# DMA transposes that read SBUF instead of a copy in DRAM, in a macaron block with an S4D layer

## The chip, the cores and the metric

The kernel runs on one core of a Trainium2 chip. The metric is the device time of one execution in microseconds (us). A core has a matrix engine (TensorE; PE in the profile, its weight loads PEld), a vector engine (VectorE, DVE), a scalar engine (ScalarE, ACT), GpSimd (POOL) and a sync engine (SP) that only issues transfers. Each has its own in-order queue of instructions; a DMA is issued from such a queue (SPq, ACTq, POOLq in the profile) and carried out by 16 DMA engines, which signal when the data has landed. SBUF is the on-chip memory of 128 partitions, PSUM holds what TensorE writes, and DRAM is off the chip's core.

## What is computed

The input `x` is 8 x 2048 x 256 in float32. Three sublayers follow each other, each added to its own input:

```python
x = x + 0.5 * ffn(layernorm(x))          # 256 -> 1024 (relu) -> 256
x = x + s4d(layernorm(x))                # below
x = x + 0.5 * ffn(layernorm(x))          # the same weights

# s4d, for each of the 256 channels h
K[h, l] = 2 * Re( sum_n Ct[h, n] * exp(dtA[h, n] * l) )       # 64 states, 2048 lags
y = causal convolution of the rows with K (the reference uses FFTs)
out = layernorm(x + y + x * D) * ln_w + ln_b
```

The kernel doesn't use FFTs. It cuts the 2048 positions into 16 chunks of 128 and computes the convolution by a table inside a chunk and by 64 complex states carried from chunk to chunk. For that it builds, for every pair of channels, tables of powers of exp(dtA) in two orientations: one is called P here, the other is P transposed.

## The kernel before, in words

**Sublayers.** The two feed-forward sublayers, `a` and `b`, run through the same function `sublayer`. A group `g` is 256 rows (two tiles of 128); there are 64 groups. A group takes 8 steps, one for each 128 of the 1024 hidden columns. In a step TensorE does six matmuls `up` (line 854: two halves of the depth times three products of high and low parts, by which float32 accuracy is reached), ACT makes the high part `hh` of the relu from PSUM (line 926), DVE the low part `hl` (line 116 is the helper that records it), and TensorE does the six matmuls `down` (line 864) of the step three steps earlier (`LAG = 3`). So ACT and DVE have about three steps to deliver a pair before TensorE stands still for it.

**Beside it**, generators advance by one `yield` in each step: `pre` prepares the rows of a later group (load, layer norm, transposition, split into `xh` and `xl`) and starts 18 (`a`) or 19 (`b`) steps before its group; `post` adds the result and, in sublayer `a`, normalizes the rows a second time into `u`, the input of the S4D layer. Most ACT and DVE instructions that are to keep their place in the queue are pinned behind what was traced before them (`keep_in_program_order`); the rest are ordered by the scheduler.

**Rows transposed in two ways.** Groups below `DMA_A = 44` in `a` and below `DMA_B = 2` in `b` are transposed on TensorE (line 794). The 20 groups of `a` from 44 on and the 62 groups of `b` from 2 on go through `turn_by_dma`: the float32 rows `xn` are split into two planes of 16-bit halves (`pl`, line 815, plane 0 on DVE, plane 1 on ACT), the planes are stored to DRAM (`xp`, line 819), three steps later a transposing DMA reads them back (`pt`, line 823), three steps after that DVE and ACT put the halves together again (`xf`, line 833, pinned), and `xh` and `xl` follow one and two steps later (lines 835 and 837). The tiles `pl`, `pt` and `xf` share one pair of buffers in rotation.

**The batches of P.** While sublayer `a` runs, a background generator (`matrices`) makes the tables. It is called at a pace in us: a cycle of its main loop is `PA = 9.1` of that pace in the first part and `PB_ = 10.3` in the second, cut into six sub-steps. There are 32 batches of 8 channels. In cycle `bt`, four generators advance together, each for its own batch:

- `make(bt)` computes P of the batch on POOL, six instructions, in place in a quarter of `u` that isn't filled yet (`room`).
- `spread(bt - 1)` waits two sub-steps (`DI`), copies the two 16-bit planes of P into `planes[:, bt % 2]` on ACT (line 620, pinned, one plane per sub-step, sub-steps 2 and 3), stores them to `pv_dram` (line 623, sub-step 4), and stores P itself to `o_dram` (line 625).
- `turn(bt - 2)` issues, at sub-step 2 of the next cycle, the transposing DMA from `pv_dram` back into the same half of `planes` (line 631, pinned on SP).
- `transpose(bt - 3)` puts the planes together again over P's own place (line 646: plane 0 on DVE, plane 1 on ACT, both pinned) at sub-step 0, and stores the result to `pt_dram` (line 650).

`planes` has two halves, taken in turn by the batches. The loop has 32 + `BACK` cycles with `BACK = 3`. A fourth generator, `lags`, runs along and makes the tables inside a chunk.

**After sublayer a** the states are computed from `pt_dram`, scanned over the chunks, and the outputs computed from `o_dram` (lines 1064 to 1178); then sublayer `b` follows.

Of the kernel before, what the change touches and what calls it, by code (L numbers as in the profile page):

```python
# [13 lines left out]
U16 = mybir.dt.uint16  # L14
# [5 lines left out]
P = 128  # L20
# [23 lines left out]
def macaron_s4d_kernel(  # L44
# [17 lines left out]
    nc = tc.nc  # L62
    V = nc.vector
    A_ = nc.scalar
# [3 lines left out]
    N = c_re.shape[1]  # L68
# [5 lines left out]
    NDC = H // P  # L74
    NFC = W // P
    NTB = 2
# [8 lines left out]
    PINT = 1  # L85
# [7 lines left out]
    BCH = 8  # L93
    NBT = H // BCH
# [6 lines left out]
    dram = ctx.enter_context(tc.tile_pool(name="dram", bufs=1, space=DRAM))  # L101
    ps = ctx.enter_context(tc.tile_pool(name="ps", bufs=2, space=PSUM))
    upool = ctx.enter_context(tc.tile_pool(name="upool", bufs=1))
    wpool = ctx.enter_context(tc.tile_pool(name="wpool", bufs=1))
# [4 lines left out]
    def bank(tag, name):  # L109
        return ps.tile([P, 512], F32, name=name, tag=tag, bufs=BANKS[tag])  # L110

    def slot(tag, shape, name, dtype=F32):
        return work.tile(shape, dtype, name=name, tag=tag, bufs=BUFS[tag])
# [99 lines left out]


    o_dram = [dram.tile([P, BCH * P], F32, name=f"o_{i}") for i in range(NBT)]
    pv_dram = [dram.tile([P, 2 * BCH * P], U16, name=f"pv_{i}") for i in range(2)]
    pt_dram = [dram.tile([P, BCH * P], F32, name=f"pt_{i}") for i in range(NBT)]
    kpad = dram.tile([H, KROW], F32, name="kpad")

# [38 lines left out]
    def matrices():  # L258
# [24 lines left out]
        for i, src in enumerate(raw + [dtx]):  # L283
            pt = bank("b", f"ptr{i}")
# [22 lines left out]
        r = zim  # L307
# [24 lines left out]
        f, a = r, z  # L332
# [133 lines left out]
        for i in range(H // P):  # L466
            nc.gpsimd.dma_start(
                out=kpad[i * P : (i + 1) * P, P + 1 :], in_=zeros[:, 0 : P - 1]
# [6 lines left out]
        with nc.allow_non_contiguous_dma(reason="256 numbers"):  # L475
            nc.gpsimd.dma_start(
                out=kpad.rearrange("(g c) k -> c g k", c=2)[:, :, P], in_=k0
# [100 lines left out]
        def p_of(bt):  # L578

            r, i = (room[2], 28 + bt % 4 * 8) if bt < first else (room[3], (16, 24, 48, 56)[bt % 4])  # L580
            return r[:, i * P : (i + 8) * P]
# [5 lines left out]
        def make(bt):  # L587

            E = G_
            pp = p_of(bt).rearrange("p (r g k) -> p r g k", r=2, g=PB)  # L590
            tm = tmp_of(bt)
            gs = slice(bt * PB, (bt + 1) * PB)
            br, bi = (
                pb[:, ri, gs, ::-1].unsqueeze(2).to_broadcast([P, PB, NA, NB]) for ri in range(2)
            )
            ar, ai = (
                pa[:, ri, gs, ::-1].unsqueeze(3).to_broadcast([P, PB, NA, NB]) for ri in range(2)
            )
            pr, pi = (pp[:, ri].rearrange("p g (a b) -> p g a b", b=NB) for ri in range(2))
            E.tensor_mul(pr, br, ar)  # L600
            yield
            E.tensor_mul(tm, bi, ai)
            yield
            E.tensor_sub(pr, pr, tm)
            yield
            E.tensor_mul(pi, br, ai)
            yield
            E.tensor_mul(tm, bi, ar)
            yield
            E.tensor_add(pi, pi, tm)  # L610
            yield

        def spread(bt):

            pl = planes[:, bt % 2]
            pu = p_of(bt).bitcast(U16).rearrange("p (m w) -> p w m", w=2)
            for _ in range(DI):
                yield
            for w in range(2):
                tc.keep_in_program_order(A_.copy(pl[:, w], pu[:, w]))  # L620
                yield
            via = pv_dram[bt % 2]
            nc.sync.dma_start(out=via, in_=pl.rearrange("p w m -> p (w m)"))
            yield
            nc.sync.dma_start(out=o_dram[bt], in_=p_of(bt))
            yield

        def turn(bt):
            for _ in range(PX):
                yield  # L630
            ins = nc.sync.dma_start(
                out=planes[:, bt % 2].rearrange("p w (k n) -> p (w k) n", n=P),
                in_=pv_dram[bt % 2], transpose=True,
            )
            if PINT:
                tc.keep_in_program_order(ins)
            yield

        def transpose(bt):
            pl, ptb = planes[:, bt % 2], p_of(bt)  # L640
            for _ in range(PY):
                yield
            pu = ptb.bitcast(U16).rearrange("p (c l r n w) -> p w r l c n", c=2, r=2, n=N, w=2)
            plv = pl.rearrange("p w (r l c n) -> p w r l c n", r=2, c=2, n=N)
            for w in range(2):
                ins = P_REINT[w](pu[:, w], plv[:, w])
                if PPIN:
                    tc.keep_in_program_order(ins)
            yield
            nc.sync.dma_start(out=pt_dram[bt], in_=ptb)  # L650
            yield

        planes = wpool.tile([P, 2, 2, BCH * P], U16, name="planes", tag="wE")
        P_REINT = (V.tensor_copy, A_.copy)
        PY = 0
        BACK = 3
        DI = 2
        PX = 2
        PA = 9.1
        PB_ = 10.3  # L660
        PPIN = 1

        beside = lags()
        for bt in range(NBT + BACK):
            parts = []
            if 0 <= bt - BACK < NBT:
                parts.append(transpose(bt - BACK))
            if 0 <= bt - 2 < NBT:
                parts.append(turn(bt - 2))
            if 0 <= bt - 1 < NBT:  # L670
                parts.append(spread(bt - 1))
            if bt < NBT:
                parts.append(make(bt))
            for n in range(6):
                for p in parts:
                    next(p, None)
                next(beside, None)
                yield (PA if bt < first + BACK else PB_) / 6
            if bt == first + BACK - 1:
                yield "half"  # L680
# [71 lines left out]
    def ffn_in(xt, name, on_act=NTB, by_dma=False, joint=None):  # L752
# [36 lines left out]
        if by_dma:  # L789
            return (yield from turn_by_dma(xn, name, Y2 - 1 if joint else Y2))  # L790
# [14 lines left out]
        V.tensor_sub(xl, ptv, xh.bitcast(F32))  # L805
        return xh, xl

    xp_dram = [dram.tile([P, 2 * NDC * NTB * P], U16, name=f"xp_{i}") for i in range(4)]

    def turn_by_dma(xn, name, y2):  # L810

        pl = slot("pl", [P, 2, NDC, NTB, P], f"pl_{name}", U16)
        xu = xn.bitcast(U16).rearrange("p i (d c w) -> p d i c w", d=NDC, w=2)
        for w, copy in DEINT:
            copy(pl[:, w], xu[:, :, :, :, w])  # L815
        yield
        via = xp_dram[turned_[0] % 4]
        turned_[0] += 1
        nc.sync.dma_start(out=via, in_=pl.rearrange("p w d i c -> p (w d i c)"))
        for _ in range(Y1):  # L820
            yield
        pt = slot("pl", [P, 2, NDC * NTB * P], f"pt_{name}", U16)
        nc.sync.dma_start(
            out=pt.rearrange("p w (k t) -> p (w k) t", t=P), in_=via, transpose=True
        )
        for _ in range(y2):
            yield
        xh = slot("xh", [P, NDC, TOK], f"xh_{name}", F32R)
        xl = slot("xl", [P, NDC, TOK], f"xl_{name}", F32R)
        xf = slot(XF, [P, NDC, TOK], f"xf_{name}")  # L830
        xv = xf.bitcast(U16).rearrange("p d (t w) -> p (d t) w", w=2)
        for w, copy in REINT:
            tc.keep_in_program_order(copy(xv[:, :, w], pt[:, w]))
        yield
        A_.copy(xh, xf)
        yield
        V.tensor_sub(xl, xf, xh.bitcast(F32))
        return xh, xl

    Y1, Y2 = 3, 3  # L840
    XF = "pl"
    DEINT = (0, V.tensor_copy), (1, A_.copy)
    REINT = (0, V.tensor_copy), (1, A_.copy)
    DMA_A = 44
    DMA_B = 2
    turned_ = [0]

    def up(wt, xT, ph, fc):
        xh, xl = xT
# [385 lines left out]
    def begin():  # L1235
        for _ in range(sizes[1] // PB):
            next(head)

    sublayer(
        w1t, w2t, pre_a, post_a, 18, "a", load_weights(), chain(matrices(), early()),  # L1240
        {"half": NG // 2, "tables": NG * 3 // 4},
        {NG * SLOTS - 6: lambda: next(head), NG * SLOTS - 1: begin},
# [127 lines left out]
```

## Time and profile before

| | |
|---|---|
| median of 3 runs | 1764.35 us (1762.26 to 1765.85) |
| the profiled execution's own time | 1761.45 us |
| its span, first to last instruction | 1759.6 us |
| TensorE busy | 1724.2 us, 98% |
| VectorE busy | 1373.7 us, 78% |
| ScalarE busy | 986.3 us, 56% |
| GpSimd busy | 588.7 us, 33% |
| moved by DMA | 242.68 MB; the SP queue's packets took 41.1% of 16 engines' span |
| transposing DMAs | 32 for P (`planes<-pv`), 20 and 62 for rows (`pt_a<-xp`, `pt_b<-xp`) |
| stores that feed them | 32 of 512 KB (`pv<-planes`), 82 of 256 KB (`xp<-pl`) |

Sublayer `a` lasts until about 806 us of the span, the S4D layer until about 1010, sublayer `b` to the end. The batches of P lie between 220 and 597 us.

In the rows of the profile, a name such as `planes<-pv` is output and input of a transfer, `L646` a line of the kernel, `x32` a count. In a table by windows each engine has its busy time and, in brackets, the number of its instructions in the stretch; PEclk is the TensorE clock that was granted, as a share of full speed, and the last two columns are the busy share of the DMA engines and what they moved in GB/s. In waits, the three numbers are us in total, times, and the longest. In the chain (the work that ended last, followed back from the end) the two numbers ahead are start and duration.

### The profile page before, as it was taken

What the parts mean: (1) busy time and instruction counts of PE and PEld (TensorE: products, weight loads), DVE (VectorE), ACT (ScalarE), POOL (GpSimd) and SP (SyncE); (2) the same over time, 40 slices, a digit from 0 to 9 for tenths busy, and PEclk for the clock granted to TensorE, in tenths of its full rate; (3) what the DMA queues carried; (4) which work ended last, traced back from release to release, by engine and by line L of the source; (5) the groups of instructions that cost most, each with busy time, mean ns of one, the idle gap of its engine ahead of it and who ended that gap; (6) DMA issues with size and microseconds to landing.
All of it is one profiled execution on the core that took longest, in us unless ns stands there. A gap on an engine that the chain in (4) does not pass through costs nothing.

```text
span 1759.6 us, 40994 instructions
## 1 busy us (share of the span) xinstructions
PE 1724.2 (98%) x15367; PEld 1697.3 (96%) x15367; DVE 1373.7 (78%) x4405; ACT 986.3 (56%) x2178; POOL 588.7 (33%) x550
## 2 busy tenths in 40 slices
PE   9999999989999999999999799999999999999998
PEld 7999999989999999999999799999999999999998
DVE  6998877767776667766999788888888888888884
ACT  4555467667777755544555445555555555555553
POOL 1117989875775115111000122222222222222220
PEclk9999999999999999999999999999999999999999
DMA  5111177669768633246888913333333333333331
GB/s 189 49 37 52 48 214 227 215 185 269 246 218 243 167 101 99 91 111 197 265 261 261 277 55 91 97 91 95 89 94 91 95 92 95 86 97 91 95 92 49
DMA packets 293277, 242.68 MB, mean 138 GB/s; under 512 B 164564, under 2 KB 237012, under 8 KB 292566
## 3 DMA queue, kind: packets, MB, share of 16 engines
q1 hardware_dynamic: 265648, 206.36, 41.1%
q10 hardware_dynamic: 26502, 32.52, 5.4%
q8 instruction: 120, 1.97, 0.4%
q0 software_dynamic: 928, 1.19, 0.3%
q14 instruction: 79, 0.65, 0.1%
HBM read 91.89 MB, written 109.84 MB: 115 GB/s over the span
## 4 chain that ended last, share of the span: by engine, by line
PE 64%; DVE 10%; DMA 3%; issue 1%; ACT 1%; POOL 0%; SPq 0%; ACTq 0%; DVEq 0%; POOLq 0%
PE ph_b L854 21%; PE po_b L864 21%; PE po_a L864 10%; PE ph_a L854 10%; DVE e L1127 2%; DVE te L1128 2%; DMA planes<-pv 1%; DVE xsB L1130 1%; DVE xsA L1130 1%; DVE xsA L1129 1%; DVE xsB L1129 1%; PE py L1172 1%; DVE xsE L1130 0%; DMA pt_a<-xp 0%; DMA xp<-pl_a 0%
## 5 line engine op out<-in xcount | busy, mean ns | idle before, releaser
L864 PE MATMUL po_a<-wa,hx_a 128*128 128x256 f32 x3072 | 456.7, 285 | 11.4 <-DVE hx_a L116 11.2
L854 PE MATMUL ph_a<-xh_a,wa 128*128 128x256 f32 x2048 | 457.0, 287 | 0.8 <-ACT xh_a L803 0.7
L854 PE MATMUL ph_b<-xh_b,wb 128*128 128x256 f32 x2048 | 442.8, 284 | 0.7 <-ACT xh_b L803 0.7
L864 PE MATMUL po_b<-wb,hx_b 128*128 128x256 f32 x3072 | 441.4, 283 | 2.0 <-DVE hx_b L116 2.0
L864 PEld LDWEIGHTS po_a<-wa,hx_a 128*128 128x128 f32 x3072 | 407.2, 192 | 13.8 <-DVE hx_a L116 13.1
L864 PEld LDWEIGHTS po_b<-wb,hx_b 128*128 128x128 f32 x3072 | 400.5, 192 | 2.4 <-DVE hx_b L116 2.4
L854 PEld LDWEIGHTS ph_a<-xh_a,wa 128*128 128x128 f32 x2048 | 356.4, 193 | 3.6 <-ACT wa L194 1.5
L854 PEld LDWEIGHTS ph_b<-xh_b,wb 128*128 128x128 f32 x2048 | 353.0, 193 | 1.1 <-ACT xh_b L803 1.1
L926 ACT ACTIVATE hx_b<-ph_b 128x256 fp32r<-128x256 f32 x512 | 192.0, 381 | 241.5 <-PE ph_b L854 222.9
L926 ACT ACTIVATE hx_a<-ph_a 128x256 fp32r<-128x256 f32 x512 | 194.9, 387 | 236.0 <-PE ph_a L854 222.0
L116 DVE SCALAR_TENSOR_TENSOR hx_a<-ph_a,hx_a 128x256 fp32r<-128x256 f32 x512 | 209.8, 414 | 125.5 <-ACT hx_a L926 123.2
L854 PE MATMUL ph_a<-xl_a,wa 128*128 128x256 f32 x1024 | 290.7, 285 | 0.0
L854 PE MATMUL ph_b<-xl_b,wb 128*128 128x256 f32 x1024 | 285.3, 284 | 0.0
L1305 POOL TENSOR_TENSOR xb<-xb,lnb_sb 128x512 f32<-128x512 f32 x64 | 82.6, 1292 | 504.8 <-DMA xb<-x_dram 342.4
L116 DVE SCALAR_TENSOR_TENSOR hx_b<-ph_b,hx_b 128x256 fp32r<-128x256 f32 x512 | 210.3, 414 | 52.3 <-ACT hx_b L926 46.3
L854 PEld LDWEIGHTS ph_a<-xl_a,wa 128*128 128x128 f32 x1024 | 198.0, 193 | 0.8 <-DVE xl_a L805 0.4
L854 PEld LDWEIGHTS ph_b<-xl_b,wb 128*128 128x128 f32 x1024 | 197.7, 193 | 0.0
L777 POOL TENSOR_TENSOR xa<-xa,hb 128x512 f32<-128x512 f32 x64 | 88.6, 1384 | 282.2 <-ACT xn L730 252.0
L777 POOL TENSOR_TENSOR xb<-xb,hb 128x512 f32<-128x512 f32 x64 | 95.1, 1486 | 55.2 <-ACT xn L730 23.5
L730 ACT ACTIVATE xn<-xb,nb_fb,t_fb 128x255 f32<-128x255 f32 x127 | 69.5, 594 | 76.4 <-DVE nb_fb L116 76.4
L815 DVE COPY pl_b<-xn 128x512 uint16<-128x512 uint16 x62 | 44.5, 717 | 73.3 <-ACT xn L730 73.3
L730 ACT ACTIVATE u<-xa,nb_u,t_u 128x256 f32<-128x256 f32 x104 | 90.1, 866 | 0.0
(263 smaller groups left out, 2511.9 us busy)
## 6 DMA issues: line engine op xcount, KB each, us to landing
o<-u SPq DMA_DIRECT2D x32, 512.0 KB, 3.4
pv<-planes SPq DMA_DIRECT2D x32, 512.0 KB, 3.6
pt<-u SPq DMA_DIRECT2D x32, 512.0 KB, 3.7
tz<-kpad SPq DMA_DIRECT2D x64, 256.0 KB, 4.7
xb<-x_dram SPq DMA_DIRECT2D x64, 256.0 KB, 2.7
out_dram<-xb SPq DMA_DIRECT2D x64, 256.0 KB, 2.9
x_dram<-xa ACTq DMA_DIRECT2D x62, 256.0 KB, 2.0
xp<-pl_b SPq DMA_DIRECT2D x62, 256.0 KB, 2.0
```

Of the source, the lines that this page charges most:

```text
L116: return V.scalar_tensor_tensor(out=o, in0=a, scalar=s, in1=b, op0=op0, op1=op1)
L730: ins = A_.activation(dst, src, AF.Identity, bias=nb[:, i : i + 1], scale=rs[:, i : i + 1])
L777: return G_.tensor_add(xt, xt, hb2.unsqueeze(1).to_broadcast([P, NTB, H]))
L815: copy(pl[:, w], xu[:, :, :, :, w])
L854: nc.tensor.matmul(ph, wt[wp][:, dc, fs], xp[:, dc, :], start=(n == 0), stop=(n == 3 * NDC - 1))
L864: nc.tensor.matmul(po[:, i, :], hp[:, tsl], wt[wp][:, fc, :], start=(fc == 0 and i == 0 and n == 0), stop=(fc == NFC - 1 and n == 2), skip ...
L926: last[A_] = A_.activation(hh, ph, AF.Relu)
L1127: E.tensor_mul(t1, xv[:, :, :, j, :], wr_b)
L1128: E.tensor_mul(t2, xv[:, ::-1, :, j, :], wi_b)
L1129: E.tensor_add(xv[:, :, :, j + 1, :], xv[:, :, :, j + 1, :], t1)
L1130: E.tensor_add(xv[:, :, :, j + 1, :], xv[:, :, :, j + 1, :], t2)
L1305: G_.tensor_add(xt, xt, lnb_sb.unsqueeze(1).to_broadcast([P, NTB, H]))
```

## The change

The planes are no longer stored to DRAM; the transposing DMA takes its input from SBUF. For P, the tile that held two alternating halves now holds `planes` (what is to be turned) and `turned` (what has been turned), one of each for all batches. `turn` is gone: `spread` issues the transposing DMA, pinned, at sub-step 4, right after the two copies. `transpose` waits four sub-steps and puts the planes together at sub-step 4 of the cycle after that; `BACK` falls from 3 to 2. For the rows, the transposing DMA is issued one step after the copies into `pl`, where the store was, and `Y2 = 6` steps lie between it and the copies that put the halves together, so that these keep their step.

```diff
-    pv_dram = [dram.tile([P, 2 * BCH * P], U16, name=f"pv_{i}") for i in range(2)]
...
         def spread(bt):
 
-            pl = planes[:, bt % 2]
             pu = p_of(bt).bitcast(U16).rearrange("p (m w) -> p w m", w=2)
-            for _ in range(DI):
+            yield
+            yield
+            for w in range(2):
+                tc.keep_in_program_order(A_.copy(planes[:, w], pu[:, w]))
                 yield
-            for w in range(2):
-                tc.keep_in_program_order(A_.copy(pl[:, w], pu[:, w]))
-                yield
-            via = pv_dram[bt % 2]
-            nc.sync.dma_start(out=via, in_=pl.rearrange("p w m -> p (w m)"))
+            tc.keep_in_program_order(nc.sync.dma_start(
+                out=turned.rearrange("p w (k n) -> p (w k) n", n=P),
+                in_=planes.rearrange("p w m -> p (w m)"), transpose=True,
+            ))
             yield
             nc.sync.dma_start(out=o_dram[bt], in_=p_of(bt))
             yield
 
-        def turn(bt):
-            for _ in range(PX):
-                yield
-            ins = nc.sync.dma_start(
-                out=planes[:, bt % 2].rearrange("p w (k n) -> p (w k) n", n=P),
-                in_=pv_dram[bt % 2], transpose=True,
-            )
-            if PINT:
-                tc.keep_in_program_order(ins)
-            yield
-
         def transpose(bt):
-            pl, ptb = planes[:, bt % 2], p_of(bt)
-            for _ in range(PY):
+            ptb = p_of(bt)
+            for _ in range(4):
                 yield
             pu = ptb.bitcast(U16).rearrange("p (c l r n w) -> p w r l c n", c=2, r=2, n=N, w=2)
-            plv = pl.rearrange("p w (r l c n) -> p w r l c n", r=2, c=2, n=N)
+            plv = turned.rearrange("p w (r l c n) -> p w r l c n", r=2, c=2, n=N)
             for w in range(2):
-                ins = P_REINT[w](pu[:, w], plv[:, w])
-                if PPIN:
-                    tc.keep_in_program_order(ins)
+                tc.keep_in_program_order(P_REINT[w](pu[:, w], plv[:, w]))
             yield
             nc.sync.dma_start(out=pt_dram[bt], in_=ptb)
             yield
 
-        planes = wpool.tile([P, 2, 2, BCH * P], U16, name="planes", tag="wE")
+        both = wpool.tile([P, 2, 2, BCH * P], U16, name="planes", tag="wE")
+        planes, turned = both[:, 0], both[:, 1]
         P_REINT = (V.tensor_copy, A_.copy)
-        PY = 0
-        BACK = 3
-        DI = 2
-        PX = 2
+        BACK = 2
...
-            if 0 <= bt - 2 < NBT:
-                parts.append(turn(bt - 2))
...
-    xp_dram = [dram.tile([P, 2 * NDC * NTB * P], U16, name=f"xp_{i}") for i in range(4)]
-
     def turn_by_dma(xn, name, y2):
...
             copy(pl[:, w], xu[:, :, :, :, w])
         yield
-        via = xp_dram[turned_[0] % 4]
-        turned_[0] += 1
-        nc.sync.dma_start(out=via, in_=pl.rearrange("p w d i c -> p (w d i c)"))
-        for _ in range(Y1):
-            yield
         pt = slot("pl", [P, 2, NDC * NTB * P], f"pt_{name}", U16)
         nc.sync.dma_start(
-            out=pt.rearrange("p w (k t) -> p (w k) t", t=P), in_=via, transpose=True
+            out=pt.rearrange("p w (k t) -> p (w k) t", t=P), in_=pl.rearrange("p w d i c -> p (w d i c)"),
+            transpose=True,
         )
         for _ in range(y2):
             yield
...
-    Y1, Y2 = 3, 3
+    Y2 = 6
```

More of the change, by code (lines that the diff above doesn't have):

```diff
@@ L651, in transpose @@
             yield
-        planes = wpool.tile([P, 2, 2, BCH * P], U16, name="planes", tag="wE")
+        both = wpool.tile([P, 2, 2, BCH * P], U16, name="planes", tag="wE")
+        planes, turned = both[:, 0], both[:, 1]
         P_REINT = (V.tensor_copy, A_.copy)
-        PY = 0
-        BACK = 3
-        DI = 2
-        PX = 2
+        BACK = 2
         PA = 9.1
         PB_ = 10.3
-        PPIN = 1
         beside = lags()
@@ L845, in macaron_s4d_kernel @@
     DMA_B = 2
-    turned_ = [0]
     def up(wt, xT, ph, fc):
```

## The prediction

> **What bounds the kernel now.** I read the page's engine shares first, then a table by windows, then the chain, the waits, and the order of the SP and ACT queues.
>
> ```profile
> PE 1724.2 (98%) x15367; PEld 1697.3 (96%) x15367; DVE 1373.7 (78%) x4405; ACT 986.3 (56%) x2178; POOL 588.7 (33%) x550
> ```
>
> TensorE is the bound, and the change takes no instruction from it. A gain can only come from TensorE's holes, a loss only from new ones. So I looked for holes in windows of 20 us (the six that matter, and two undisturbed ones):
>
> ```profile
> 340.00:360.00 20.00, 16.89 (x130) 16.69 (x129) 18.28 (x35) 13.35 (x25) 16.15 (x17) 0.91 0.70 221
> 380.00:400.00 20.00, 15.24 (x122) 15.04 (x121) 8.75 (x27) 10.71 (x20) 13.23 (x12) 0.89 0.94 212
> 400.00:420.00 20.00, 20.00 (x160) 20.00 (x160) 15.62 (x41) 17.77 (x33) 14.99 (x12) 0.94 0.97 303
> 440.00:460.00 20.00, 20.00 (x170) 20.00 (x169) 14.68 (x42) 16.45 (x32) 16.58 (x15) 1.00 0.88 283
> 560.00:580.00 20.00, 17.69 (x146) 17.38 (x145) 11.38 (x36) 15.39 (x30) 2.93 (x2) 1.00 0.73 196
> 580.00:600.00 20.00, 19.62 (x162) 19.22 (x161) 14.45 (x48) 15.23 (x31) 1.91 (x3) 1.00 0.80 223
> 1020.00:1040.00 20.00, 18.03 (x151) 17.83 (x150) 16.20 (x63) 9.03 (x23) 4.09 (x3) 1.00 0.20 53
> 1060.00:1080.00 20.00, 20.00 (x169) 20.00 (x168) 16.40 (x58) 10.80 (x26) 5.49 (x4) 1.00 0.36 97
> ```
>
> An undisturbed window holds 170 matmuls, so one takes 0.118 us. A window's price is its missing matmuls by that, which takes in the lower clock (0.89 and 0.94 of full speed) that follows a standstill. From 1040 to 1740 us there is no hole. What ended the holes stands in the chain:
>
> ```profile
> 378.84 6.68 DMA planes<-pv
> 387.41 9.56 DMA planes<-pv
> ...
> 566.70 3.46 DMA xp<-pl_a
> 570.18 4.11 DMA pt_a<-xp
> ...
> 1034.20 3.44 DMA pt_b<-xp
> ```
>
> Three of the four holes end behind a transposing DMA. (a) At 393 to 398 us DVE and ACT stand at line 646 for the transposition that took 9.56 us; 48 + 10 matmuls are missing, 6.8 us. (b) At 575 us they stand for a row transposition that could start only when the store before it had landed; 24 + 8 missing, 3.8 us. (c) At 351 to 354 us the chain shows a tiny DVE instruction (`q_u`) of 3.08 us beside busy POOL, no transfer; 40 missing, 4.7 us. (d) At 1037 us the first DMA-turned group of sublayer `b` comes late; 18 or 19 missing, 2.1 us. The waits say that ACT and DVE also stand where TensorE doesn't notice:
>
> ```profile
> ACT u L646 <- DMA planes<-pv: 18.1, 8, 7.0
> DVE u L646 <- DMA planes<-pv: 12.9, 6, 6.5
> ACT xf_b L833 <- DMA pt_b<-xp: 30.7, 42, 1.6
> ```
>
> The last line costs nothing: 42 waits of some 0.7 us lie in the stretch without holes. A stall of ACT of 1.75 us at 383.9 us also left TensorE running, one of 3.3 us at 571 us cost it 2.3 us. About three steps of 1.44 us are the cover.
>
> **The change part by part.**
>
> *The stores go.* 32 of 512 KB and 82 of 256 KB, 38 MB of the 242.68. Issuing one takes SP 0.34 us, which nobody waits for. What counts is DMA time: between 200 and 600 us the queues moved 86.7 MB at a busy share of 0.73, and the P stores are 16.8 MB of it, 19%, so about 0.6 is left. It also takes away the store's landing ahead of each row transposition:
>
> ```profile
> o<-u SPq DMA_DIRECT2D x32, 512.0 KB, 3.4
> pv<-planes SPq DMA_DIRECT2D x32, 512.0 KB, 3.6
> ...
> xp<-pl_b SPq DMA_DIRECT2D x62, 256.0 KB, 2.0
> ...
> pt_b<-xp SPq DMA_TRANSPOSE x62, 3.5
> ...
> planes<-pv SPq DMA_TRANSPOSE x32, 6.0
> ```
>
> *The transposition from SBUF.* No row shows one. For 512 KB, the floor is a plain store from SBUF, 3.6 us to landing; the ceiling is the longest transposition in the chain, 9.56. From DRAM the 32 took 4.4 us when little else ran (at 262 us) and 6.0 in the median. I take 5.5: the same work, less traffic beside it, no reason in the trace why the source should matter. For 256 KB, floor 2.0, ceiling 5.6 (3.5 scaled by 9.56/6.0); taken 3.5.
>
> [...] The trace has only the DRAM form, 1.24 us on SP for a group and 1.3 to 6.2 (median 3.1) for P. [...]
>
> *P's order.* Until now a transposition had its own half of `planes`; pinned behind the store of line 650, it started 0.4 us after line 646 of the batch before and had the rest of the cycle, some 8.5 of 10 us. Now two things hold it. It writes `turned`, so SP waits for line 646 of the batch before (DVE 0.97 us, ACT 1.37), issued in the same sub-step; queued behind on SP are the `pt` store, which waits for the same, the `o` store, and from group 44 on the rows' transpositions, which have slack. And it reads the only `planes`, so the next batch's first copy (line 620, pinned on ACT) waits until it has landed, with the relus of line 926 queued behind, and DVE and TensorE behind those. From sub-step 4 to the next sub-step 2 are four sub-steps of 10.1/6 us, 6.7 us, less 1.5 for line 646: room for 5.2 us in the first 18 cycles, and some 6.8 later, where copies 11.9 us apart (481.4 and 493.4 us) show a longer cycle. With 5.5 us ACT waits 0.3 us in early cycles and nothing later. ACT was busy 80 of 105 us from 440 to 545, so it has 2.7 us free in a cycle (3.1 between 225 and 275): covered. If that cover goes, the relus come late and TensorE stands.
>
> *The rest of P.* Line 646 comes two sub-steps (3.4 us) sooner. It overwrites P in place, so `o` must have landed: five sub-steps, 8.4 us, against 3.4 to landing. POOL's wait for the `pt` store (35.6 us in ten waits) shrinks; POOL isn't the bound. The loop has one cycle less, some 10 us sooner at both marks, for which nobody waits. Copies and stores that stay are as many as before.
>
> *The rows.* `pl` to `xf` was 5.4 us in the trace (1053.5 to 1058.85) and holds its place; in it lay store, landing and transposition, now the transposition alone: 3.5 us, 1.9 to spare. The shared buffer asks that the group before has done line 837, at 1061.4, ahead of the next copies at 1063.4. So (b) and (d) go; what is late next there is nothing that the trace shows.
>
> *The sum.* (a) 6.8, (b) 3.8 and (d) 2.1 go: 12.7 us. (c) stays at 4.7: its cause isn't in the change, though its neighbours move; it could vanish or double. Against it I set one new hole of the size of (b), 3.8 us, for a batch in which P's copy, row loads and row transpositions meet. Net 8.9: the profiled execution's 1761.45 us (span 1759.6, 1.85 around it) becomes 1752.5, and the median of the runs, 2.9 above it, 1755.5.
>
> **The rivals.**
>
> *The transposition from SBUF is slow, and ACT becomes the pace of sublayer a (slower).* Place: the first copy of each batch, line 620. ACT's free time is used up at 5.2 + 2.9, about 8.1 us in the first 18 cycles, and 6.8 + 2.7, 9.5, in the other 14; beyond, each us costs one us a cycle. At 9.56 us: 18 x 1.5 + 14 x 0.1 = 28 us. A group's transposition at 5.6 stays hidden, so (b) and (d) still give 5.9: 1786. For it: one buffer instead of two, and the row of 9.56. Against it: that row fell where the DMA engines were 94% busy, and a fifth of the traffic goes.
>
> *The gain is eaten.* Transpositions of 7 to 8 us leave ACT under its limit, but waits of 2 to 3 us meet the queue at a bad moment in one of four batches, at half of (b)'s 2.3 us: 8 x 1.15, some 9 us with the clock behind it, and (a) is only moved. Net 12.7 - 6.8 - 9: 1767, or 1760 if (a) goes all the same. For it: 8 of 32 waits at line 646 were long already.
>
> *Re-sorted queues open a hole elsewhere.* Unpinned transfers and DVE work find new places; a second (c) and a second (a) cost 11.5 us and cancel the gain: 1767. Against it: the pinned ACT and DVE order is nearly the same.
>
> *Nothing is gained.* The holes come from other meetings of the same transfers and stay: 1764.
>
> **How the numbers follow.** Chances: forecast 0.53 (its own range 1747 to 1761: all four holes gone is 17.4 us, less is 3); slow transposition 0.18 (1770 to 1800, more at the edge); eaten 0.16; re-sorted 0.08; nothing 0.05. The range for 8 in 10 leaves out some 5 in 100 below 1747 and the worst part of the slow case above 1788. A change of under 0.2%, 3.5 us, can't be told from none. The forecast gives 0.50 of faster and 0.03 of same; eaten 0.04, 0.05 and 0.07; re-sorted 0.01, 0.03 and 0.04; nothing 0.04 of same and 0.01 of slower; the slow case 0.18 of slower. That is 0.55, 0.15 and 0.30.
>
> **What would show it.** Right: the P transpositions land in 5 to 6 us; windows near 393, 575 and 1037 us hold 169 or 170 matmuls; the waits of `xf_b` vanish; a new wait of ACT at line 620 for the transposition, under 1 us each; DMA share near 0.6. Wrong: transpositions above 8 us, that wait of 2 us or more in most batches, relus waited for by DVE and TensorE between 220 and 590 us, or a clock below 1.00 in more windows than three.

## The result, and the profile after

The change made the kernel slower: 1775.4 us in the median of 6 runs (1768.64 to 1777.16), beside 1765.16 us for the kernel before in 6 runs. The ratio is 1.0055, with a 95% interval of 1.0037 to 1.0073, so 0.55% slower. The forecast was 1755.5, faster; the time lies in the stated range, but on the other side of the time before. The profiled execution took 1776.07 us, its span 1774.3, 14.7 more than the span before.

TensorE is still the bound and has the same 15367 matmuls; the page's line of the engines, after:

```profile
PE 1729.7 (97%) x15367; PEld 1700.2 (96%) x15367; DVE 1386.4 (78%) x4405; ACT 984.9 (56%) x2178; POOL 591.4 (33%) x550
```

What went as forecast is the transfers. The page's counts of bytes went from 242.68 to 204.39 MB, the SP queue's share from 41.1% to 35.2%, and the issues of transposing DMAs show these medians to landing (last number, us):

```profile
pt_b<-pl_b SPq DMA_TRANSPOSE x62, 3.1
...
planes<-planes SPq DMA_TRANSPOSE x32, 5.0
...
pt_a<-pl_a SPq DMA_TRANSPOSE x20, 3.1
```

The 512 KB of P land in 5.0 us (4.3 to 7.1), not in 6.0 as from DRAM, and a group's 256 KB in 3.1, not in 3.3 to 3.5. So the cause isn't a slow transposition. The table by windows shows where TensorE lost its time; here are the prediction's windows between 340 and 600 us that had holes, and those that have them now:

```profile
280.00:300.00 20.00, 18.32 (x152) 17.92 (x151) 17.50 (x37) 11.97 (x25) 14.50 (x15) 1.00 0.47 133
300.00:320.00 20.00, 17.38 (x144) 16.98 (x143) 14.62 (x33) 13.61 (x27) 19.61 (x21) 1.00 0.58 160
...
340.00:360.00 20.00, 17.68 (x143) 17.04 (x142) 12.55 (x27) 13.58 (x23) 11.96 (x14) 1.00 0.83 215
360.00:380.00 20.00, 12.80 (x89) 12.80 (x90) 16.22 (x32) 9.73 (x20) 10.21 (x10) 0.74 0.42 129
380.00:400.00 20.00, 20.00 (x170) 20.00 (x169) 13.70 (x38) 14.99 (x29) 15.45 (x13) 1.00 0.47 127
400.00:420.00 20.00, 18.84 (x153) 18.23 (x152) 14.71 (x39) 14.79 (x28) 16.95 (x14) 1.00 0.91 279
420.00:440.00 20.00, 16.97 (x128) 16.64 (x127) 11.26 (x33) 14.19 (x26) 9.10 (x9) 0.91 0.61 174
...
560.00:580.00 20.00, 19.58 (x163) 19.38 (x162) 12.36 (x38) 14.23 (x30) 14.48 (x12) 1.00 0.79 185
580.00:600.00 20.00, 17.41 (x143) 17.00 (x142) 12.97 (x41) 15.81 (x31) 1.54 (x1) 1.00 0.63 145
```

The old hole (a) at 393 to 398 us is filled, but 280 to 320, 360 to 380 and 420 to 440 us have new ones, and 580 to 600 a larger one. The same table in coarse windows gives 1581 and 1973 matmuls before in 200:400 and 400:640, and 1522 and 1916 after: 59 + 57 fewer, 116 x 0.118 = 13.7 us. The S4D layer's first output matmul is 14.1 us later (839.7 against 825.6 us), so the whole loss arises while P is made. Of what is left, the S4D layer took 2.7 us longer (179.7 against 177.0 us from its first output matmul to its last), for which the versions below give 176.3 to 180.6, the rows' half alone 179.4; its cause stays open. Hole (d) gave back 2.0 (TensorE's wait for `hx_b` at line 839 is 0.0, it was 2.0 at line 864).

What ended the new holes stands in the chain of after:

```profile
336.34 5.59 DMA planes<-planes
...
345.30 4.31 DMA planes<-planes
...
352.98 5.37 DMA planes<-planes
...
358.47 1.76 DVE u L635
360.23 6.58 DVE q_u L116
...
423.28 5.72 DMA planes<-planes
...
586.56 7.14 DMA planes<-planes
```

Two kinds: P's transpositions, and one tiny DVE instruction, `q_u`, as in hole (c) of before, but twice as long. The waits of after (us in total, times, longest):

```profile
PE po_a L839 <- DVE hx_a L116: 21.7, 16, 7.4
...
ACT planes L618 <- DMA planes<-planes: 19.9, 13, 3.4
...
DVE u L635 <- DMA planes<-planes: 9.2, 6, 2.7
...
ACT u L635 <- DMA planes<-planes: 2.7, 2, 1.6
...
ACT xf_b L809 <- DMA pt_b<-pl_b: 2.2, 1, 2.2
```

The wait of the copies (line 618, line 620 before) is new: in 13 places, 1.5 us in the mean. The wait of `xf_b` fell from 30.7 to 2.2 us, and gained nothing by it, as nobody waited for it.

**How one batch holds the next.** ACT's timeline from 347 to 362 us, with what ended the idle time before in brackets:

```profile
347.56 0.43 ACT L901 ACTIVATE hx_a<-ph_a 128x256 fp32r<-128x256 f32 x1
349.71 1.99 ACT L618 COPY planes<-u 128x1024 uint16<-128x1024 uint16 x2 [1.72 <-DMA planes<-planes]
...
351.61 1.35 ACT L635 COPY u<-planes 128x1024 uint16<-128x1024 uint16 x1
352.83 0.36 ACT L901 ACTIVATE hx_a<-ph_a 128x256 fp32r<-128x256 f32 x1
...
358.43 1.99 ACT L618 COPY planes<-u 128x1024 uint16<-128x1024 uint16 x2 [2.60 <-DMA planes<-planes]
360.32 1.33 ACT L635 COPY u<-planes 128x1024 uint16<-128x1024 uint16 x1
361.53 0.36 ACT L901 ACTIVATE hx_a<-ph_a 128x256 fp32r<-128x256 f32 x1
```

The transposition that was issued at 345.30 lands at 349.61 and lets the next batch's two copies start at 349.71. Right behind them stands the putting together of the batch that has just landed (line 635), until 352.96, and at 352.98 the next transposition is issued. That is a closed ring through the single `planes` and `turned`: 4.3 to 5.4 us of transposition, then 3.3 us of ACT, so 7.7 (345.30 to 352.98) and 8.7 us (to 361.68) per batch, with no slack anywhere in it. Between the relus at 347.56 and 352.83 ACT made none for 4.8 us, and from 355.8 to 361.5 none for 5.7; TensorE has about 4.3 us of cover, by the prediction's estimate (three steps of 1.44 us). It stood 0.89 us at 345 and 1.24 us at 352.5, by its own timeline.

The batches enter this ring in bunches. The transpositions of P were issued at 308.3, 336.3, 345.3, 353.0, 361.7, 388.8, 396.9, 404.7, 414.0 and 423.3 us: gaps of 27 to 28 us and then several batches 7.7 to 9.3 us apart. For the first 18 batches the prediction reckoned with an even cycle of 10.1 us; their mean distance here is 12.2. Such bunches were there before the change too, where the smallest distance was 6.0 us:

```profile
341.03 1.32 SPq L631 DMA_TRANSPOSE planes<-pv  x1
...
347.04 3.72 SPq L631 DMA_TRANSPOSE planes<-pv  x1
```

**The other kind.** At 360 us DVE and POOL show, in the timeline of after:

```profile
360.13 6.68 DVE L116 SCALAR_TENSOR_TENSOR q_u<-q_u,s_u 128x4 f32<-128x4 f32 x1
366.73 0.41 DVE L116 SCALAR_TENSOR_TENSOR hx_a<-ph_a,hx_a 128x256 fp32r<-128x256 f32 x1
...
359.57 1.75 POOL L603 TENSOR_TENSOR u<-u 128x512 f32<-128x512 f32 x1
361.29 1.04 POOL L599 TENSOR_TENSOR u<-u 128x512 f32<-128x512 f32 x1
...
365.75 1.04 POOL L607 TENSOR_TENSOR u<-u 128x512 f32<-128x512 f32 x1
367.25 1.05 POOL L599 TENSOR_TENSOR u<-u 128x512 f32<-128x512 f32 x1 [0.47 <-DVE t_u L699]
```

An instruction on 128 x 4 numbers, 0.16 us in the median, took 6.68 us, as long as POOL went from one instruction to the next without a pause; it ended when POOL's pause began. TensorE waited 7.40 us for the `hx_a` queued behind it. The two kinds meet here: the piece ahead of `q_u` in the chain is DVE's copy of line 635, which had itself waited 1.95 us for the transposition. With a `q_u` of 0.16 us TensorE would have gone on at about 360.8 us at the earliest, after 1 us, by an estimate from these rows. So at most 6.4 us are `q_u`'s. With the clock of 0.74 after it the window 360:380 lacks 80 matmuls, 9.5 us. The same happened to a `q_u` at 283.7 us (3.53 us) and to DVE's copy of line 635 at 315.5 us (3.38 us; its median is 0.99), both beside unbroken POOL work.

**The two kinds in one account.** TensorE's idle times in sublayer `a` from 200 to 640 us, each put down to what had held up the chain last (in brackets, where it ended):

| | before | after |
|---|---|---|
| all | 11.45 us | 21.49 us |
| a tiny DVE instruction or copy beside POOL | 3.11 (354 us) | 1.49 (289), 1.35 (319), 7.40 (367): 10.24 |
| P's transposition, and the ACT work that follows its landing | 4.76 (398 us) | 1.26 (309), 0.89 (346), 1.24 (354), 3.03 (433), 1.68 (596): 8.10 |
| a row transposition | 2.31 (577 us) | none |
| others | 1.27 | 3.15 |

So the gain of (b) is there, and both other kinds grew, by 7.1 and 3.3 us.

### The profile page after: what moved, and what is told of

It reads as the page before. It is cut to its first block, busy times and chain, and to the rows that moved or that the text cites. A ratio compares the mean times of both kernels' runs of the same rounds, so it can differ in the third digit from the quotient of the medians.

```text
span 1774.3 us, 40643 instructions
## 1 busy us (share of the span) xinstructions
PE 1729.7 (97%) x15367; PEld 1700.2 (96%) x15367; DVE 1386.4 (78%) x4405; ACT 984.9 (56%) x2178; POOL 591.4 (33%) x550
## 2 busy tenths in 40 slices
DMA packets 276859, 204.39 MB, mean 115 GB/s; under 512 B 162740, under 2 KB 235188, under 8 KB 276150
## 3 DMA queue, kind: packets, MB, share of 16 engines
q1 hardware_dynamic: 249232, 168.08, 35.2%
## 4 chain that ended last, share of the span: by engine, by line
PE 65%; DVE 12%; DMA 4%; ACT 2%; issue 1%; POOL 0%; ACTq 0%; DVEq 0%; SPq 0%
PE ph_b L829 21%; PE po_b L839 21%; PE po_a L839 11%; PE ph_a L829 11%; DMA planes<-planes 3%; DVE e L1102 2%; DVE te L1103 2%; DVE xsB L1105 1%; DVE xsA L1105 1%; DVE q_u L116 1%; DVE xsA L1104 1%; DVE xsB L1104 1%; DMA xa<-in_L_attn_x_dram 1%; ACT u L635 1%; PE py L1147 1%
## 5 line engine op out<-in xcount | busy, mean ns | idle before, releaser
L795 DVE COPY pl_b<-xn 128x512 uint16<-128x512 uint16 x62 | 30.7, 494 | 74.1 <-ACT xn L712 74.1
```

## The experiments

Each ratio is against the kernel before, run beside it on the same chip, with its 95% interval. "Missing matmuls" is the sum of what the windows of 20 us between 200 and 640 us lack of 169; before it was 135, after 247. "TensorE's idle time" is that of the table above, 11.45 and 21.49 us.

### Which half loses

The rows' part of the diff alone (`turn_by_dma`, `Y2 = 6`), and P's part alone (`spread`, `transpose`, `BACK`):

> Only the rows' half of the change: groups turned by DMA read their planes from SBUF, the batches of P go through DRAM as before. If the loss lies in P's half, the holes at 575 and 1037 us go and nothing is added: 5.9 us less than before, about 1759 us, and the waits of xf_b for the transposition fall from 30.7 us to under 3. If the rows' half shares in the loss (a transposition that waits on SP for the group before, or one that holds up P's), it is 1765 us or more.

> Only P's half of the change: P's planes are turned out of SBUF, with one buffer for what is to be turned and a cycle less; the rows go through DRAM as before. If the loss lies in P's half, it is slower than the whole change by what the rows gain, 1777 to 1781 us, with ACT's waits at the copies into planes near 20 us as after the change. If the loss needs both halves on one SP queue, it is near before, 1763 to 1767 us.

Rows alone: 1758.64 us, ratio 0.9975 (0.9964 to 0.9986), 89 missing, TensorE's idle time 7.64 us. P alone: 1776.41, ratio 1.0075 (1.0055 to 1.0096), 221 missing, idle 19.68, with nearly every idle time of after's list at its place, the 7.40 us (at 366.8) among them. The waits of P alone show the same new line as after, and the old wait of the rows:

```profile
ACT xf_b L815 <- DMA pt_b<-xp: 36.3, 46, 1.7
...
ACT planes L618 <- DMA planes<-planes: 18.6, 10, 3.0
```

So the rows' half gained 4.0 us, where (b) and (d) had been put at 3.8 + 2.1 = 5.9, and P's half lost 13.8. They hardly act on each other: 13.8 - 4.0 = 9.8, and the whole change lost 10.2.

### Is it the ring?

First the putting together two sub-steps earlier, so that `turned` comes free before the next copies:

```diff
         def transpose(bt):
             ptb = p_of(bt)
-            for _ in range(4):
+            for _ in range(2):
                 yield
```

> The whole change, but a batch of P is put together at sub-step 2 instead of 4, ahead of the next batch's copies, so that the transposing DMA finds turned free when its planes are copied. The time from a transposition's issue to the next copy grows from some 5 us to 6.7. Theory wait: ACT's waits at the copies into planes (19.9 us in 13) fall under 8 us, the holes at 346, 433 and 590 us (some 96 missing matmuls, 11 us) shrink by half or more: 1767 to 1771 us. Theory port: these waits may fall, but the long q_u remain, and the time stays within 3 us of the change's 1775.

1767.73 us, ratio 1.0023 (1.0009 to 1.0037), 177 missing. The waits of this run:

```profile
ACT u L635 <- DMA planes<-planes: 25.9, 14, 4.4
...
DVE u L635 <- DMA planes<-planes: 16.1, 12, 2.5
...
ACT planes L618 <- DMA planes<-planes: 0.6, 1, 0.6
```

The wait only moved, from the copies to the putting together, but half of the loss went, as the theory of the wait expected (5.1 us are left of 10.2; idle 12.55 us). It didn't go where that theory looked for it: the windows at 340 and 420 us still lack 29 and 33 matmuls (26 and 41 in after). What shrank is the hole at 360 us (44 for 80) and the one at 590, which is gone. The ring is shorter, but ACT still stands in it.

Then a second `planes`, in cells of `room[2]` that are idle until they are filled, for the odd batches of the first half; `turned` stays single:

```diff
+        other = room[2][:, 20 * P : 28 * P].bitcast(U16).rearrange("p (w m) -> p w m", w=2)
...
+            pl = other if bt % 2 and bt < first else planes
...
-                tc.keep_in_program_order(A_.copy(planes[:, w], pu[:, w]))
+                tc.keep_in_program_order(A_.copy(pl[:, w], pu[:, w]))
...
-                in_=planes.rearrange("p w m -> p (w m)"), transpose=True,
+                in_=pl.rearrange("p w m -> p (w m)"), transpose=True,
```

(the table `kev` moved from cell 20 to cell 15 of `room[2]` for it)

> The whole change, but in the first 16 batches those with an odd number have a second planes buffer, in cells of u that are idle then (a small table of the lags moves to make room). Nothing else is moved. Theory loop: with one buffer, a transposition, the next two copies, the join and the next transposition are one closed ring of 5.0 + 2 x 1.05 + 1.4 us and the relus between them, some 10 us, longer than the 7.7 to 9 us in which batches follow each other where POOL catches up (340 to 365 and 390 to 435 us); with two, the ring is 5.0 + 1.4. Then ACT's waits at the copies fall from 19.9 us to under 6, the holes of these stretches shrink by half, 1760 to 1767 us. Rival order (the loss is where the join and the transposition now lie in the queues, at sub-step 4): within 3 us of the change's 1775.

And the early putting together with one transposing DMA for each plane, right behind its copy:

```diff
             for w in range(2):
                 tc.keep_in_program_order(A_.copy(planes[:, w], pu[:, w]))
                 yield
+                tc.keep_in_program_order(nc.sync.dma_start(
+                    out=turned[:, w].rearrange("p (k n) -> p k n", n=P),
+                    in_=planes[:, w], transpose=True,
+                ))
-            tc.keep_in_program_order(nc.sync.dma_start(
...
-            ))
...
-            for _ in range(4):
+            for _ in range(2):
```

> The whole change with P put together at sub-step 2, and each plane turned by a DMA of its own right after its copy, so that each half of planes and of turned is free after its own, shorter transposition; 32 transpositions more. Theory loop: the ring for a plane is some 3.1 + 1.05 + 1.4 us and never closes; 1757 to 1764 us, ACT's waits for transpositions under half of those with the join at sub-step 2 alone (25.9 us). Rival cost (each transposition costs the same, whatever its size, so two cost more DMA and SP time than one): above that kernel's 1767.7 us.

Second buffer: 1759.05 us, ratio 0.9972 (0.996 to 0.9984), 122 missing; its waits (line 619 is line 618 of after):

```profile
ACT planes L619 <- DMA planes<-planes: 9.5, 8, 2.7
...
ACT u L636 <- DMA planes<-planes: 4.3, 3, 2.5
...
DVE u L636 <- DMA planes<-planes: 3.5, 2, 2.0
```

Split: 1762.4 us, ratio 0.998 (0.9966 to 0.9994), 132 missing; the copies wait 0.7 us in all, the putting together 20.7 on ACT and 9.5 on DVE, and the halves land in 4.2 us. Both remove the whole loss of P's half, or nearly (the rows' half alone is at 0.9975), and leave the source in SBUF and the missing cycle as they are in the change. The second buffer doesn't touch the sub-steps of P's schedule either, only who waits for whom, and with it two transpositions are issued 5.9 us apart (340.52 and 346.37), closer than the old ring allowed. So at this pace the loss comes from the single buffers. Both kinds of idle time shrink with them: it is 9.81 and 9.52 us, none over 1.6 us with the second buffer and one of 2.76 with the split, although a `q_u` of 3.48 and a copy of 4.82 us beside POOL occur with the second buffer and a `q_u` of 3.95 with the split. Why no such instruction meets a row of the ring's waits there, as at 358 to 367 us in after, is a matter of timing that these runs don't separate further. The expectation for the sizes of the waits was missed twice (9.5 us, where under 6 was expected; 20.7, where under half of 25.9 was): a wait's total doesn't give its price, its place does.

### Is it DVE beside POOL?

`q_u` and `nb_u` have three instructions with two tensors from SBUF. In this version each became four instructions on one column, with the second tensor as a number per partition:

```diff
-        stt(q, q, 0.25, s, ALU.mult, ALU.add)
+            for i in range(n):
+                ts(q[:, i : i + 1], q[:, i : i + 1], 0.25, ALU.mult, s[:, i : i + 1], ALU.add)
```

(the other two in the same way)

> The whole change, but the three tiny DVE instructions of a group's norm in sublayer a that read two tensors in SBUF (q_u twice, nb_u, 128x4) are four each with one tensor and per-partition scalars. Theory port: in the changed kernel q_u stands 3.5 us at 284 us and 6.6 us at 360 us behind POOL's back-to-back work, and this is most of the loss; then these instructions take 0.2 us each, the holes at 284, 360 and 405 us (116 missing matmuls, 13.7 us) go, less some 1 us a group of added DVE time that is hidden: 1762 to 1766 us. Theory wait (ACT's copies that wait for the only planes buffer): 1773 to 1778 us, as the change.

1773.74 us, ratio 1.0057 (1.0039 to 1.0075), 220 missing, idle 15.56 us: no gain beside the 1.0055 of the change, and the theory that this kind alone makes the loss is missed. Its rows by tile (ns, shortest, median and longest), between 200 and 620 us:

```profile
L119 DVE TENSOR_SCALAR q_u<-mv_j,t_u x132: 196/204/215, 207.2 to 619.6; 128x1 f32<-128x1 f32 x132
```

and its waits:

```profile
DVE u L635 <- DMA planes<-planes: 20.8, 14, 2.1
...
ACT planes L618 <- DMA planes<-planes: 18.7, 13, 2.7
...
ACT u L635 <- DMA planes<-planes: 15.9, 10, 3.4
```

The long stalls did go: none of the 391 instructions took over 0.22 us. But the ring's waits on DVE and ACT at line 635 rose from 11.9 to 36.7 us: what had held up DVE had perhaps also spaced out the batches. The test is not clean. Twelve instructions of 0.20 us are more work for DVE than three of 0.16 (1396.1 us busy against 1386.4), and P's first transposition is issued at 241.2 us instead of 224.9, the last at 595.2 instead of 600.0, so the batches lie 11.4 us apart in the mean instead of 12.1. With the second buffer under it:

> The whole change with the second planes buffer in the first 16 batches, and q_u and nb_u as instructions with one tensor. With the change as it is, this rewriting gained nothing, though the instructions that stood behind POOL were gone; the time came back as waits for transpositions. Theory loop: with the ring open, what the rewriting frees is no longer taken up: 3 to 6 us under the second buffer alone (1759), 1753 to 1757. If these short stalls of DVE cost TensorE nothing, or the added instructions cost as much, 1758 to 1763.

1770.75 us, ratio 1.004 (1.0025 to 1.0055), 206 missing, where the second buffer alone has 1759.05 and 122. So the rewrite itself costs some 12 us, a clear miss. The waits at its line 636 for transpositions rise with it from 12.4 us (ACT and DVE, both buffers) to 33.5. Here too P starts later, with its first transposition at 241.5 us instead of 224.5; whether this makes the loss was not tested.

### Is it the bunches?

The pace of the first part slower by 0.8 us a cycle, with the whole change:

```diff
-        PA = 9.1
+        PA = 9.9
```

> The whole change with PA = 9.9 instead of 9.1: a cycle of P in the first part is asked for 9% later, which the cycle saved at the end pays for. Theory loop: more time for the ring, ACT's waits at the copies fall under 12 us, 1764 to 1771 us. If the batches follow each other closely because POOL falls behind and catches up, and not because of the pace asked for, the waits stay and so does the time, 1773 to 1778 us.

1758.07 us, ratio 0.9974 (0.9956 to 0.9991), 108 missing, idle 7.89 us: 17 us below after by one number, and better than either expectation. The copies' waits are nearly as before (17.4 us in 12), against the expectation, but 280 to 440 us is almost free of holes. What is left stands in two windows and in ACT's timeline of this run:

```profile
300.00:320.00 20.00, 20.00 (x170) 19.92 (x169) 17.00 (x42) 14.96 (x29) 19.85 (x19) 1.00 0.61 195
...
360.00:380.00 20.00, 20.00 (x169) 20.00 (x170) 15.36 (x42) 13.98 (x28) 16.75 (x15) 1.00 0.69 197
...
540.00:560.00 20.00, 15.41 (x120) 14.39 (x119) 15.49 (x33) 12.69 (x24) 13.74 (x12) 1.00 0.51 123
560.00:580.00 20.00, 18.82 (x135) 18.82 (x136) 15.49 (x40) 15.33 (x30) 9.96 (x9) 0.83 0.72 190
```

```profile
553.17 1.05 ACT L618 COPY planes<-u 128x1024 uint16<-128x1024 uint16 x1 [3.74 <-DMA planes<-planes]
```

The transpositions are now issued at 309.0, 321.3, 340.6, 348.2, 359.5, 373.1 and 381.9 us; only one gap is as small as the 7.7 to 8.7 us of above. The hole in the last two windows is the ring again, in a longer form: a transposition issued at 546.50 lets the copies start at 553.17, DVE ends line 635 at 560.83, and the next transposition is issued at 560.90, 14.4 us after the one before. And no `q_u` or `nb_u` takes over 1.99 us, although they take 84.3 us in all, more than in after (78.5): which suggests, but doesn't show, that the two kinds of hole have the bunches in common. To see what the pace is worth without the change, it was set in the kernel before, with the rows' half, and with the second buffer of above:

> The kernel before with PA = 9.9 instead of 9.1 and nothing else: a control for the run of the change with that pace, which took 17 us off the change. Theory loop: before, the ring of single buffers isn't there, the wider pace has little to give and the loop of 35 cycles, not 34, runs closer to its marks: 1762 to 1768 us. If the wider pace helps any kernel by keeping POOL, DVE and ACT from meeting in bunches, it gains 5 us or more here too: under 1760 us.

> The rows' half of the change with the batches of P through DRAM, and PA = 9.9. The rows' half alone was 0.25% under before. Theory loop: the pace adds nothing, 1756 to 1763 us; if the pace helps by itself, 1750 to 1755.

> The whole change with the second planes buffer in the first 16 batches and PA = 9.9. Theory loop: both undo the same loss, so together they give little more than one, 1753 to 1759 us. If they undo two losses (the ring, and POOL's bunches that hold up DVE), the gains add: under 1750 us.

The kernel before with this pace: 1752.4 us, ratio 0.9938 (0.9922 to 0.9955), 48 missing, idle 3.74 us; no `q_u` over 2 us. So the pace helps by itself, against the expectation of the theory of the ring, which had it do nothing here, and what it took off the change isn't proof of the ring. The rows' half with it: 1748.39 us, ratio 0.9914 (0.99 to 0.9929), 20 missing, idle 1.12 us: the best of all, and below both ranges expected. The second buffer with it, in the range that the theory of the ring expected: 1755.28, ratio 0.9958 (0.9942 to 0.9975), 90 missing, of which 57 in one window that the rows' half has full. That window of the second buffer with the pace, and ACT's timeline in it:

```profile
540.00:560.00 20.00, 15.50 (x112) 14.55 (x111) 15.61 (x30) 13.63 (x25) 13.03 (x12) 0.88 0.56 136
```

```profile
550.65 1.05 ACT L619 COPY planes<-u 128x1024 uint16<-128x1024 uint16 x1 [3.76 <-DMA planes<-planes]
```

and the same window of the rows' half with the pace, where P goes by DRAM and two buffers:

```profile
540.00:560.00 20.00, 20.00 (x169) 20.00 (x168) 16.62 (x48) 17.90 (x34) 12.81 (x10) 1.00 0.84 225
```

The second buffer exists in the first half only; in the second half the ring of one is back, with the same wait of 3.7 us as in the version with the pace alone. Last, the split with the pace, which opens the ring in both halves:

> The whole change, with P put together at sub-step 2, one transposing DMA of 256 KB for each plane right behind its copy, and the first part's cycle at 9.9 instead of 9.1. Theory (the ring copy, transposition, putting together through the single pair of buffers costs only where it is slower than the distance of two batches): the ring is open by the split and the batches are apart by the pace, so that the hole of the windows 540 to 580 us that the pace alone and the second buffer with the pace left (83 and about 60 missing matmuls there) is gone as well; the copies of line 618 wait under 3 us in total, under 60 matmuls are missing between 200 and 640 us, and the time is 1747 to 1753 us, as the rows' half with this pace (20 missing, 1748.4). Rival (transposing P from SBUF costs something by itself, by more ACT and SP work in a batch or the putting together in fewer sub-steps): over 80 missing matmuls and 1755 us or more.

1757.58 us, ratio 0.9963 (0.995 to 0.9975), 103 missing. The copies no longer wait for a transposition at all, and the two windows of the second half lack 35 matmuls instead of 83, but smaller holes stand elsewhere: one ends behind an `nb_u` of 4.70 us beside POOL at 285 us, one behind a transposition of 7.42 us at 347 us, for which the early putting together waits, others at 392 and 560 us behind copies and small DVE work. By its numbers the rival of this run was right: with P from SBUF the kernel stays above the rows' half alone at the same pace, by 9.7 us with single buffers, 6.9 with the second buffer and 9.2 with the split. So at this pace opening the ring gains little, unlike at 9.1, where the second buffer took away the whole loss of P's half. Whether the rest comes from having fewer buffers or is a cost of its own stays open; a full second buffer in both halves was not tried.

## Why the prediction was wrong

*The stores go, and the traffic.* Right: 38 MB less, and the DMA engines' busy share between 200 and 600 us fell from 0.73 to 0.59, where about 0.6 was forecast.

*The transposition from SBUF.* Right, and a little pessimistic: 5.0 us where 5.5 was taken, 3.1 where 3.5 was. The rival of the slow transposition named the place that lost, the first copy of each batch, and gave 1786; but its condition, a transposition above 8.1 us, was not met (7.1 at most).

*P's order.* Here is the step that failed: "With 5.5 us ACT waits 0.3 us in early cycles and nothing later", and "covered". It set the transposition against four sub-steps of an even cycle of 10.1 us. The batches do not come evenly: after a gap of 27 us they come 7.7 to 9.3 us apart, and there the ring itself is the pace. Instead of 0.3 us the copies waited 1.5 in the mean and 3.4 at most. And the cover was the wrong one: ACT's free time in a cycle (2.7 us) was compared with the wait, but what counts is how long no relu passes. The wait, two copies and the putting together now stand in one row, 1.7 + 2.0 + 1.3, about 5 us, against TensorE's 4.3. Before, these stood at sub-step 0 and at sub-steps 2 and 3; the change put the one behind the other two, which the prediction told and didn't add up.

*The sum.* (a) went at its place: the window 380:400 is full. (b) went with the rows' half; near its place, at 594 us, now stands P's transposition of 7.14 us. (d) went: 2.0 us. The term "(c) stays at 4.7" was wrong. In place of 3.11 us TensorE stands 10.24 us behind this kind (1 us of it or more the ring's, by the estimate above), and the windows 280:300, 300:320 and 360:380, where it stands, lack 17 + 25 + 80 = 122 matmuls, 14.4 us with the clock (300:320 also holds 1.26 us of the ring). Of the reason given, "its cause isn't in the change", the runs show the contrary: P's half alone brings the 7.40 us, and opening the ring, or the slower pace, takes them away. Why they do stays open. "One new hole of 3.8 us" was five waits in the ring, 8.10 us; the windows 340, 400, 420 and 580 lack 26 + 16 + 41 + 26 = 109 matmuls, 12.9 us. So 14.4 + 12.9 = 27.3 us stand where the forecast had 4.7 + 3.8 = 8.5, which is 18.8 more; with the S4D layer's 2.7 that makes 1774.0 of its 1752.5, and 1776.07 was measured in this execution.

*The rivals.* The nearest was "re-sorted queues", a second (c) and a second (a), which still came out at 1767 with a chance of 0.08. Its mechanism happened, twice over. Its argument against, that the pinned order is nearly the same, asked for the wrong thing: the order changed little, the distances did. "The gain is eaten" wanted waits of 2 to 3 us in one batch of four at the copies; 13 waits of 1.5 us is near that, but without the slow transposition that it put them down to.

*The rows.* Right in mechanism, a third too large: 4.0 us by the medians instead of 5.9.

## What to carry to other kernels

Before a buffer is taken from a pair, add up the ring that the one left closes (transfer, then each instruction that must follow it, up to the next transfer's issue) and compare it with the smallest distance of two batches in the trace, not with the mean cycle. Here the prediction's 5.5 us, with the two copies of 1.05 us and line 646 of 1.37 us in the trace of before, give a ring of 9.0 us, and the same trace had distances of 6.0 to 8.9 us in six places. On ACT the wait and the work pinned behind it counted together (1.7 + 2.0 + 1.3 us at 348 to 353 us of after), against the cover of the engine that is the bound (here about 4.3 us, by the estimate above). And where background work comes in bunches, try its pace first: one number was worth 0.6% here without any other change.

## What the runs showed of the hardware

`q_u`, a DVE instruction with two tensors from SBUF (128 x 4), took 0.16 us in the median of after and up to 6.68 us while POOL ran on SBUF without a pause. Written with one tensor and a number per partition, in a kernel with the same POOL instructions, `q_u` and `nb_u` never took over 0.22 us between 200 and 620 us (391 instructions). One tensor alone didn't keep a DVE instruction short: the copy of line 635, which has one input, took 3.38 us beside POOL at 315.5 us of after, where its median is 0.99. The stall of 6.68 us ran over six POOL instructions of 1.0 to 1.75 us, not one.

For P, a transposing DMA from SBUF was cheaper than from DRAM on SP as well as in landing: it took SP 1.98 us in the median (1.32 to 4.43), where the DRAM form took 3.09 (1.32 to 6.23), and landed in 5.0 us instead of 6.0. In the version with the rows' half alone, with P still from DRAM and less traffic than before, it was 2.90 and 5.9. For a group of rows in sublayer `b` SP took about the same from either source, 1.26 us from SBUF and 1.27 from DRAM.

A standstill of TensorE cost more than itself here: 7.40 us of TensorE at 360 us became 9.5 us of missing matmuls in a window with a granted clock of 0.74.
